# Thirty-two graph blocks through four layers on one core: bias sums, products and weight chunks take other places in the order

## The chip, the cores and the metric

The kernel runs on one core of one Trainium2 chip. Its time is the time on the device of one launch, in microseconds (us); lower is better.

## The reference

The input is x, 128 graphs of 64 nodes with 512 features, an adjacency matrix adj for each graph (symmetric in its pattern, with weights from 0.05 to 1), and a node mask of ones. Four layers follow, each with a norm, a relu and a residual; all in float32.

```python
def block(x, layer, ...):
    h = jnp.maximum(_layernorm(x, axis=-1), 0.0)
    return x + layer(h, adj, ...)

# layer 0
q, k = jnp.split(h @ Wqk, 2, axis=-1)
v = h @ Wv
agg = jnp.einsum('bij,bjd->bid', adj, k * mask[:, :, None])
w = inv_scale * mask * jnp.einsum('bid,bid->bi', q, agg)
out = jax.nn.softmax(w, axis=1)[:, :, None] * v
# layer 1: q, k, v with biases
weight = adj * jnp.exp(jnp.einsum('bqd,bkd->bqk', query, keyt))
weight = weight / jnp.sum(weight, axis=2, keepdims=True)
out = jnp.einsum('bqk,bkd->bqd', weight, value)
# layer 2: eight heads of 64, biases everywhere
scores = jnp.einsum('bhqd,bhkd->bhqk', q, k) * SCALE * (adj + adj)
out = softmax(scores) applied to v, then @ Wo.T + bo
# layer 3: graph diffusion of three hops
Xw = X @ Wv + bv
sj, si = Xw @ aw[:d, 0], Xw @ aw[d:, 0]
alpha = A * jnp.exp(leaky_relu(sj[:, None, :] + si[:, :, None] + ab[0]))
transition = alpha / (jnp.sum(alpha, axis=-1, keepdims=True) + 1e-12)
for k in range(3):
    H = H + Xk @ Wk[k] + bk[k]
    Xk = jnp.einsum('bij,bjd->bid', transition, Xk)
out = jax.nn.relu(H)
```

## The kernel before

The 8192 rows are cut into 32 blocks of 256 rows (four graphs), two tiles of 128 rows each (`TT`). `K` is 4, the number of chunks of 128 in 512 features; `F` is 256.

**Products.** A 512 x 512 weight times a block's activations is a `Product`: seven products of half size (Strassen's scheme in Winograd's form) instead of eight. VectorE and GpSimd make the sums of the operands (`sums` for the activations, `formed`, `later` and `chore` for the weights), TensorE does the seven products (L244 where the result is feature-major, L251 where it is row-major), and ScalarE, VectorE and GpSimd put the results together. A Product holds two PSUM banks, called ab and dc. Its first products are copied out (`keep_ab` L280 and L281, `keep_dc` L288), the banks take the later ones, and `store`, `store_T` or `add_to` (L302 to L341) empties them. `ps_mm` has four such banks, so the Product after the next waits until a Product's banks are empty. `ps_tr` and `ps_sc` have two banks each, for transposes and for scores and small sums.

**Order.** The program is written in the order in which blocks are to overlap: functions are generators or take lists `between`, whose entries are called at set places among the products of another block. A scheduler puts each engine's instructions in an order of its own; `tc.issue_after(i)` makes what is issued inside come after instruction i on its engine. Each engine works its list in order. All loads and stores named below go through SP's queue, in order as well: an issue that waits holds those behind it. Tiles with a tag share that tag's few buffers in turn.

**Start.** `prepare(0)` norms block 0; `transpose_weight` turns layer 0's q and k on TensorE (16 transposes, the four banks of results copied back by VectorE and ScalarE in turn, L420 and L422); `folded` multiplies them into one weight (pf, 32 matmuls, L430). `setup1` does the same for layer 1: its q and k are loaded, nine sums of products with the bias vectors are made on VectorE (L467: four for u, four for cc, one for d), then `transpose_weight` for q and for k, then `folded`. Layers 0 and 1 then run interleaved for pairs of blocks. `layer0` makes a masked adjacency am on GpSimd, its neighbour sums pa, gv, and a softmax whose end is `layer0_end`.

**Layer 2** is pipelined over blocks: `layer2_in` makes q and k of block b + 1, `layer2_scores` and `layer2_divided` its softmax, `layer2_context` and `out_part` what block b gives; the out product adds itself into x by `add_to` (L335 to L341, six operations on VectorE and GpSimd; the last on GpSimd is noted in `behind[0]`). Weight sums of later layers are done on GpSimd by `chore` (L99), one or two a block.

**Layer 3.** `setup3`, called at block 28 of layer 2, multiplies layer 3's Wv by the two halves of aw (pu, L754) to get two vectors us, stores them as a row and loads them spread over all partitions. A block then needs from Wv only four products hu (L788, two tiles by two vectors, each a sum along a row of h). `layer3_norm` loads x and adjT, norms x, makes the hu, and di and sj from them (L793, L800). `layer3_in` spreads di with a matmul (sm_i, L400), takes exp, multiplies by adjT to al (L816), then transposes h. `layer3_head` makes y2 and y1 of a block, `layer3_tail` y0 with den (L838) and the second hop (y<-po, L849), then y0's four VectorE stores (L858 to L862), `layer3_end` the last hop, the relu and out's store. In `layer3_step(b)` the norm is that of block b + 2, layer3_in that of b + 1 and layer3_end that of b - 1. The last blocks of layer 2 overlap the first of layer 3.

Of the kernel before, what the change touches and what calls it, by code (L numbers as in the profile page):

```python
# [13 lines left out]
P = 128  # L14
# [11 lines left out]
def kernel(ctx: ExitStack, tc: tile.TileContext, a: dict, out: bass.AP):  # L26
# [134 lines left out]

    def norm(x, name: str):
# [9 lines left out]
        nc.gpsimd.tensor_tensor(rstd, ve, neghalf, ALU.pow)  # L172
        nmr = small.tile([P, TT], FP, tag="nmr", name=f"nmr_{name}")
        nc.vector.scalar_tensor_tensor(nmr, mv[:, :, 0], -1.0, rstd, ALU.mult, ALU.mult)  # L174
# [48 lines left out]
    class Product:  # L223
# [109 lines left out]
        def add_to(self, x):  # L333
# [4 lines left out]
            nc.gpsimd.tensor_tensor(x[:, 1, :F], self.u3, x[:, 1, :F], ALU.add)  # L338
            nc.vector.tensor_tensor(x[:, 0, F:], self.c, x[:, 0, F:], ALU.add)
            nc.vector.tensor_tensor(x[:, 0, :F], self.a, x[:, 0, :F], ALU.add)  # L340
            nc.vector.tensor_tensor(x[:, 1, :F], self.d, x[:, 1, :F], ALU.add)  # L341
            behind[0] = nc.gpsimd.tensor_tensor(
                x[:, 1, F:], self.u3, x[:, 1, F:], ALU.add
# [67 lines left out]
    def transpose_weight(w, name: str):  # L411

        pts = [ps_mm.tile([P, K, P], FP, tag="mm", name=f"tw_{name}_{m}") for m in range(K)]
# [3 lines left out]
        for m, pt in enumerate(pts):  # L417
            flat = pt.rearrange("p k i -> p (k i)")
            if m % 2:
                nc.scalar.copy(w[:, m, :], flat)  # L420
            else:
                nc.vector.tensor_copy(w[:, m, :], flat)  # L422

    def folded(aT, bT, layer: int, place: int):

        m = slot(place, f"fold{layer}")
        for i in range(K):
# [7 lines left out]
            nc.vector.tensor_copy(m[:, quarters[i // 2][1], i % 2, :], pm[:, F:])  # L435
        return m

    def setup0():
# [4 lines left out]
        nc.vector.tensor_scalar(msc, mcol, -(float(D) ** -0.5), None, ALU.mult)  # L443
        return m, msc

    def setup1():
# [14 lines left out]
        for to, x, by in (  # L461
            *((u[:, k : k + 1], qT[:, k, :], 1) for k in range(K)),
            *((cc[:, k : k + 1], kT[:, k, :], 0) for k in range(K)),
            (d, None, 1),
        ):
            junk = med.tile([P, P, K], FP, tag="agg", name="bias1", bufs=2)
            nc.vector.scalar_tensor_tensor(  # L467
                junk, bias[:, 0] if x is None else x.rearrange("q (k p) -> q p k", k=K), 1.0,
                bias[:, by], ALU.mult, ALU.mult, accum_out=to,
            )  # L470
# [5 lines left out]
        for w, c in zip((qT, kT), "qk"):  # L476
            transpose_weight(w, f"{c}1")
        m = folded(kT, qT, 1, 2)
# [8 lines left out]
    def layer0(b: int, x, adjT, hs, hT, between):  # L487
# [3 lines left out]
        nc.gpsimd.tensor_tensor(  # L491
            am,
            adjT,
# [623 lines left out]
```

## Time and profile before

| | us |
|---|---|
| time, median of 3 runs | 2678.71 |
| lowest, highest run | 2675.41, 2680.66 |
| the profiled execution's own time | 2679.86 |
| its span | 2678.1 |
| TensorE busy in it | 2639.5 |
| VectorE, ScalarE, GpSimd busy in it | 1702.8, 947.7, 1288.7 |
| mean granted clock of TensorE | 0.996 |

The profile is of one execution: instructions of each engine with start and duration, what each waited for, and the clock granted to TensorE as a share of full speed. The page gives sums over the span. The view of waits gives, for an engine and line, the total time that it stood idle, what ended it, how many times, and the longest. The view by windows gives the busy time of PE (TensorE), PEld (its weight loads), DVE (VectorE), ACT (ScalarE) and POOL (GpSimd) in a stretch, then the granted clock, the DMA engines' share and GB/s. The timeline gives start, duration, engine, line and operation; brackets hold the idle time before it and what ended that. Names are those of the program without block numbers; q, k and v of the products are told by their suffix, as in u_y for a y product.

### The profile page before, as it was taken

What the parts mean: (1) busy time and instruction counts of PE and PEld (TensorE: products, weight loads), DVE (VectorE), ACT (ScalarE), POOL (GpSimd) and SP (SyncE); (2) the same over time, 40 slices, a digit from 0 to 9 for tenths busy, and PEclk for the clock granted to TensorE, in tenths of its full rate; (3) what the DMA queues carried; (4) which work ended last, traced back from release to release, by engine and by line L of the source; (5) the groups of instructions that cost most, each with busy time, mean ns of one, the idle gap of its engine ahead of it and who ended that gap; (6) DMA issues with size and microseconds to landing.
All of it is one profiled execution on the core that took longest, in us unless ns stands there. A gap on an engine that the chain in (4) does not pass through costs nothing.

```text
span 2678.1 us, 52780 instructions
## 1 busy us (share of the span) xinstructions
PE 2639.5 (99%) x20752; PEld 2253.1 (84%) x20752; DVE 1702.8 (64%) x4398; ACT 947.7 (35%) x2290; POOL 1288.7 (48%) x1585
## 2 busy tenths in 40 slices
PE   8999999999999999999999999999899999999999
PEld 5888888888888889999999999999777777777776
DVE  5566666666666676566566566566566666666664
ACT  2333334333333333333333333333323333333332
POOL 3443333333433335656655655655464444445544
PEclk9999999999999999999999999999999999999999
DMA  5200111111111122111111111111111111111110
GB/s 158 67 35 34 35 35 35 42 43 35 50 34 35 34 66 78 45 45 39 45 45 39 45 45 39 45 45 45 65 50 51 51 51 51 51 51 51 51 50 32
DMA packets 103165, 129.80 MB, mean 48 GB/s; under 512 B 40835, under 2 KB 50051, under 8 KB 102917
## 3 DMA queue, kind: packets, MB, share of 16 engines
q1 hardware_dynamic: 102340, 125.38, 13.9%
q8 instruction: 163, 2.67, 0.4%
q10 hardware_dynamic: 576, 1.05, 0.1%
q14 instruction: 86, 0.70, 0.1%
HBM read 76.07 MB, written 50.34 MB: 47 GB/s over the span
## 4 chain that ended last, share of the span: by engine, by line
PE 81%; POOL 6%; DVE 5%; DMA 4%; ACT 3%; issue 2%; ACTq 0%; POOLq 0%; SPq 0%; DVEq 0%
PE ab_v L251 11%; PE ab_y L251 9%; PE dc_v L251 8%; PE dc_y L251 6%; PE ab_g L244 4%; PE ab_k L244 4%; PE ab_g L251 4%; PE ab_q L244 4%; PE tr L190 3%; PE dc_g L244 3%; PE dc_g L251 3%; PE po L392 3%; PE dc_k L244 3%; PE ab_o L251 3%; PE dc_q L244 3%; DMA x<-x 2%
## 5 line engine op out<-in xcount | busy, mean ns | idle before, releaser
L179 ACT ACTIVATE h<-x,nmr,rstd 128x512 f32<-128x512 f32 x256 | 194.4, 806 | 219.6 <-DVE nmr L174 211.0
L172 POOL TENSOR_TENSOR rstd<-ve,neghalf 128x2 f32<-128x2 f32 x128 | 89.8, 701 | 365.6 <-DVE ve L170 365.4
L167 DVE BATCH_NORM_STATS2 stats<-x 128x6 f32<-128x512 f32 x256 | 165.3, 677 | 74.6 <-DMA x<-x 68.4
L251 PE MATMUL ab_y<-L_Wk,hT 128*128 128x256 f32 x768 | 207.5, 393 | 4.1 <-DVE u_y L303 2.6
L251 PEld LDWEIGHTS ab_y<-L_Wk,hT 128*128 128x128 f32 x768 | 136.4, 190 | 77.4 <-issue 25.2
L251 PE MATMUL ab_v<-L_Wv,hT 128*128 128x256 f32 x768 | 200.7, 384 | 0.0
L251 PE MATMUL ab_y<-L_Wk,S 128*128 128x256 f32 x768 | 197.8, 380 | 0.0
L251 PE MATMUL dc_v<-L_Wv,S 128*128 128x256 f32 x768 | 197.3, 379 | 0.0
L251 PE MATMUL ab_v<-L_Wv,S 128*128 128x256 f32 x768 | 197.1, 379 | 0.0
L251 PE MATMUL dc_y<-L_Wk,S 128*128 128x256 f32 x768 | 192.9, 380 | 1.3 <-DVE u_y L859 1.2
L251 PEld LDWEIGHTS dc_y<-L_Wk,S 128*128 128x128 f32 x768 | 145.2, 190 | 23.2 <-DVE u_y L859 3.7
L251 PEld LDWEIGHTS ab_v<-L_Wv,S 128*128 128x128 f32 x768 | 145.9, 190 | 19.8
L880 POOL TENSOR_TENSOR tz<-tz,y 128x512 f32<-128x512 f32 x63 | 91.5, 1452 | 146.0 <-ACT tz L877 146.0
L251 PEld LDWEIGHTS ab_y<-L_Wk,S 128*128 128x128 f32 x768 | 144.1, 191 | 18.5
L251 PEld LDWEIGHTS dc_v<-L_Wv,S 128*128 128x128 f32 x768 | 143.4, 190 | 18.9 <-issue 0.8
L251 PEld LDWEIGHTS ab_v<-L_Wv,hT 128*128 128x128 f32 x768 | 135.9, 190 | 15.4
L190 PE MATMUL tr<-ident,h 128*128 128x128 f32 x1024 | 134.4, 275 | 0.0
L190 PEld LDWEIGHTS tr<-ident,h 128*128 128x128 f32 x1024 | 119.5, 142 | 10.5
L216 POOL TENSOR_TENSOR S<-hT 128x256 f32<-128x256 f32 x128 | 101.1, 790 | 35.0 <-ACT hT L193 34.7
L219 POOL TENSOR_TENSOR S<-hT 128x256 f32<-128x256 f32 x128 | 107.9, 843 | 1.2
L306 POOL TENSOR_TENSOR gv<-u_g,p_g 128x256 f32<-128x256 f32 x32 | 23.4, 730 | 174.4 <-DVE u_g L303 174.4
L217 POOL TENSOR_TENSOR S<-S,hT 128x256 f32<-128x256 f32 x128 | 101.0, 789 | 11.6 <-DVE ve L170 10.3
(238 smaller groups left out, 6433.8 us busy)
## 6 DMA issues: line engine op xcount, KB each, us to landing
x<-x SPq DMA_DIRECT2D x128, 512.0 KB, 3.5
x<-in_x_dram SPq DMA_DIRECT2D x32, 512.0 KB, 3.6
out_dram<-x SPq DMA_DIRECT2D x31, 512.0 KB, 2.8
adjT<-in_adjT_dram SPq DMA_DIRECT2D x64, 64.0 KB, 1.9
adjq<-in_adj_dram SPq DMA_DIRECT2D x64, 64.0 KB, 2.3
L_Wk<-in_L_Wk_dram SPq DMA_DIRECT2D x16, 256.0 KB, 4.7
L_Wv<-in_L_Wv_dram SPq DMA_DIRECT2D x12, 256.0 KB, 5.3
q<-in_L_Wqk_dram ACTq DMA_DIRECT2D x4, 256.0 KB, 6.1
```

Of the source, the lines that this page charges most:

```text
L167: nc.vector.bn_stats(stats[:, t, :], x[:, t, :])
L172: nc.gpsimd.tensor_tensor(rstd, ve, neghalf, ALU.pow)
L179: nc.scalar.activation(h, x[:, t, :], AF.Relu, bias=nmr[:, t : t + 1], scale=rstd[:, t : t + 1])
L190: nc.tensor.transpose(pt[:, k, :], h[:, k * P : (k + 1) * P], ident)
L216: nc.gpsimd.tensor_tensor(S1, A21, A22, ALU.add)
L217: nc.gpsimd.tensor_tensor(S2, S1, A11, ALU.subtract)
L219: behind[0] = nc.gpsimd.tensor_tensor(S3, A11, A21, ALU.subtract)
L244: nc.tensor.matmul(dst[:, m * P : (m + 1) * P], w[:, place, k, m * P : (m + 1) * P], left[:, k, :], start=key not in self.begun, stop=last ...
L251: nc.tensor.matmul(dst, left[:, k, :], w[:, place, k, :], start=key not in self.begun, stop=last and k == 1, skip_group_check=True,)
L306: nc.gpsimd.tensor_tensor(y[:, 1, F:], self.u3, self.p5, ALU.add)
L392: nc.tensor.matmul(ps[t][half[g ^ t]], e[half[g], t, :], us[t][half[g]], start=True, stop=True)
L880: nc.gpsimd.tensor_tensor(tz[t], tz[t], y0[:, t, :], ALU.add)
```

## The change

- `setup1`: the nine bias sums are made earlier, in two groups with yields between them, so that the main loop can place them among the products of block 0; each reads a weight by columns. ScalarE copies all four banks of q's transposes; k's transposes go to `ps_tr` and `ps_sc` in turn. `layer0_end` of block 0 is called inside `folded`, after its first i.
- `transpose_weight` takes the places of its banks and which copies ScalarE does; layer 0's k uses two banks of `ps_sc` and two of `ps_mm`.
- `norm` keeps its first two small operations in `behind_norm`; msc (VectorE) and am (GpSimd) come after them.
- `add_to`: a's and d's adds come before c's; GpSimd's two adds of u3 change places.
- `setup3`: WvT is loaded as four chunks, two in one v buffer and two in agg buffers; the results of pu and pc go to two small tiles and are stored by two DMAs.
- Layer 3: `layer3_norm` is split; `layer3_dots` has the hu products, di and sj, and is issued behind the last VectorE store of y0. Both stages of `layer3_in` are called at the end of layer3_head's list. `layer3_tail` yields once more, before den. In the last three blocks of layer 2 the calls change places likewise: the first stage of layer3_in for block 0 goes into layer2_in's list, and block 2's dots come behind the last adds of out.

```diff
@@ -159,6 +159,8 @@
+    behind_norm = {}
...
@@ -169,9 +171,12 @@
         rstd = small.tile([P, TT], FP, tag="rstd", name=f"rstd_{name}")
-        nc.gpsimd.tensor_tensor(rstd, ve, neghalf, ALU.pow)
+        by_rows = nc.gpsimd.tensor_tensor(rstd, ve, neghalf, ALU.pow)
         nmr = small.tile([P, TT], FP, tag="nmr", name=f"nmr_{name}")
-        nc.vector.scalar_tensor_tensor(nmr, mv[:, :, 0], -1.0, rstd, ALU.mult, ALU.mult)
+        scaled = nc.vector.scalar_tensor_tensor(
+            nmr, mv[:, :, 0], -1.0, rstd, ALU.mult, ALU.mult
+        )
+        behind_norm.setdefault(0, (by_rows, scaled))
         hs = []
...
@@ -335,12 +340,12 @@
             nc.vector.tensor_tensor(self.u3, self.b, self.p1, ALU.add)
-            nc.gpsimd.tensor_tensor(x[:, 1, :F], self.u3, x[:, 1, :F], ALU.add)
-            nc.vector.tensor_tensor(x[:, 0, F:], self.c, x[:, 0, F:], ALU.add)
             nc.vector.tensor_tensor(x[:, 0, :F], self.a, x[:, 0, :F], ALU.add)
             nc.vector.tensor_tensor(x[:, 1, :F], self.d, x[:, 1, :F], ALU.add)
+            self.taken = nc.vector.tensor_tensor(x[:, 0, F:], self.c, x[:, 0, F:], ALU.add)
+            nc.gpsimd.tensor_tensor(x[:, 1, F:], self.u3, x[:, 1, F:], ALU.add)
             behind[0] = nc.gpsimd.tensor_tensor(
-                x[:, 1, F:], self.u3, x[:, 1, F:], ALU.add
+                x[:, 1, :F], self.u3, x[:, 1, :F], ALU.add
             )
...
@@ -408,20 +413,25 @@
-    def transpose_weight(w, name: str):
-        pts = [ps_mm.tile([P, K, P], FP, tag="mm", name=f"tw_{name}_{m}") for m in range(K)]
+    def transpose_weight(w, name: str, places=((ps_mm, "mm"),) * K, on_scalar=(1, 3)):
+        pts = [
+            pool.tile([P, K, P], FP, tag=tag, name=f"tw_{name}_{m}")
+            for m, (pool, tag) in enumerate(places)
+        ]
         for k in range(K):
...
             flat = pt.rearrange("p k i -> p (k i)")
-            if m % 2:
+            if m in on_scalar:
                 nc.scalar.copy(w[:, m, :], flat)
...
-    def folded(aT, bT, layer: int, place: int):
+    elsewhere = ((ps_tr, "tr"), (ps_sc, "sc")) * 2
+    def folded(aT, bT, layer: int, place: int, amid=lambda: None):
...
@@ -433,6 +443,8 @@
             nc.vector.tensor_copy(m[:, quarters[i // 2][1], i % 2, :], pm[:, F:])
+            if not i:
+                amid()
         return m
...
@@ -440,7 +452,8 @@
         msc = const.tile([P, n_tok // P], FP, tag="msc", name="msc")
-        nc.vector.tensor_scalar(msc, mcol, -(float(D) ** -0.5), None, ALU.mult)
+        with tc.issue_after(behind_norm[0][1].ins):
+            nc.vector.tensor_scalar(msc, mcol, -(float(D) ** -0.5), None, ALU.mult)
         return m, msc
...
@@ -458,24 +471,30 @@
         d = const.tile([P, 1], FP, tag="d1", name="d1")
-        for to, x, by in (
-            *((u[:, k : k + 1], qT[:, k, :], 1) for k in range(K)),
-            *((cc[:, k : k + 1], kT[:, k, :], 0) for k in range(K)),
-            (d, None, 1),
-        ):
-            junk = med.tile([P, P, K], FP, tag="agg", name="bias1", bufs=2)
-            nc.vector.scalar_tensor_tensor(
-                junk, bias[:, 0] if x is None else x.rearrange("q (k p) -> q p k", k=K), 1.0,
-                bias[:, by], ALU.mult, ALU.mult, accum_out=to,
-            )
+        def dots(*sums):
+            for to, x, by in sums:
+                junk = med.tile([P, P, K], FP, tag="e2", name="bias1", bufs=3)
+                nc.vector.scalar_tensor_tensor(
+                    junk, x, 1.0, bias[:, by], ALU.mult, ALU.mult, accum_out=to
+                )
+        def columns(w):
+            return [w[:, k, :].rearrange("q (k p) -> q p k", k=K) for k in range(K)]
+        dots((d, bias[:, 0], 1))
+        dots(*((u[:, k : k + 1], x, 1) for k, x in enumerate(columns(qT))))
+        yield
+        dots(*((cc[:, k : k + 1], x, 0) for k, x in enumerate(columns(kT))))
...
         nc.sync.dma_start(c1, crow.to_broadcast([P, D]))
-        for w, c in zip((qT, kT), "qk"):
-            transpose_weight(w, f"{c}1")
-        m = folded(kT, qT, 1, 2)
+        yield
+        transpose_weight(qT, "q1", on_scalar=range(K))
+        transpose_weight(kT, "k1", elsewhere)
+        m = folded(kT, qT, 1, 2, lambda: layer0_end(0, *softmax))
         formed(m, nc.gpsimd)
...
@@ -488,12 +507,13 @@
         am = small.tile([P, TT, N], FP, tag="am", name=f"am_{b}", bufs=2)
-        nc.gpsimd.tensor_tensor(
-            am,
-            adjT,
-            mcol[:, b * TT : (b + 1) * TT].unsqueeze(2).to_broadcast([P, TT, N]),
-            ALU.mult,
-        )
+        with tc.issue_after(behind_norm[0][0].ins):
+            nc.gpsimd.tensor_tensor(
+                am,
+                adjT,
+                mcol[:, b * TT : (b + 1) * TT].unsqueeze(2).to_broadcast([P, TT, N]),
+                ALU.mult,
+            )
         pa = [ps_tr.tile([P, D], FP, tag="tr", name=f"pa_{b}_{t}") for t in range(TT)]
...
@@ -738,25 +758,25 @@
         nc.sync.dma_start(ab, a["L3_ab"].to_broadcast([P, 1]))
-        halves = []
-        for i in range(2):
-            w = big.tile([P, K // 2, D], FP, tag="v", name=f"w3vT_{i}")
-            nc.sync.dma_start(
-                w,
-                a["L3_WvT"][i * D // 2 : (i + 1) * D // 2, :].rearrange("(k p) o -> p k o", p=P),
-            )
-            halves.append(w)
+        pair = big.tile([P, 2, D], FP, tag="v", name="w3vT")
+        chunks = [pair[:, k, :] for k in range(2)] + [
+            med.tile([P, D], FP, tag="agg", name=f"w3vT_{k}", bufs=2) for k in range(2, K)
+        ]
+        for k, w in enumerate(chunks):
+            nc.sync.dma_start(w, a["L3_WvT"][k * P : (k + 1) * P, :])
...
         for k in range(K):
-            for to, x in ((pu, halves[k // 2][:, k % 2, :]), (pc, bv[:, k : k + 1])):
+            for to, x in ((pu, chunks[k]), (pc, bv[:, k : k + 1])):
                 nc.tensor.matmul(to, aw[:, k, :], x, start=(k == 0), stop=(k == K - 1))
-        us2 = big.tile([2, D + 1], FP, tag="v", name="us2")
-        nc.scalar.copy(us2[:, :D], pu)
-        nc.scalar.copy(us2[:, D:], pc)
+        us2 = med.tile([2, D], FP, tag="h", name="us2", bufs=6)
+        cs2 = small.tile([2, 1], FP, tag="cc", name="cs2", bufs=1)
+        nc.scalar.copy(us2, pu)
+        nc.scalar.copy(cs2, pc)
         urow = tc.dram_tile([2, D + 1], FP, name="u3_row")
-        nc.sync.dma_start(urow, us2)
+        nc.sync.dma_start(urow[:, :D], us2)
+        nc.sync.dma_start(urow[:, D:], cs2)
         uc = const.tile([P, 2, D + 1], FP, tag="u3", name="u3")
...
@@ -775,12 +795,14 @@
         adjT = load_adjT(b, 3)
+        return x, adjT, norm(x, f"3_{b}")
+    def layer3_dots(b: int, x, adjT, hs):
         us, c3, _ = made3
-        hs = norm(x, f"3_{b}")
         sij = small.tile([P, 2, TT], FP, tag="sij", name=f"sij_{b}")
...
@@ -832,6 +854,7 @@
         p.second(ops, w3[0])
+        yield
         den = [ps_tr.tile([P, 1], FP, tag="tr", name=f"den3_{b}_{t}") for t in range(TT)]
...
@@ -859,9 +882,9 @@
         nc.gpsimd.tensor_tensor(y0[:, 1, F:], p.u3, p.p5, ALU.add)
-        nc.vector.tensor_tensor(y0[:, 0, F:], p.c, p.u2, ALU.add)
+        kept = nc.vector.tensor_tensor(y0[:, 0, F:], p.c, p.u2, ALU.add)
         nc.gpsimd.tensor_tensor(y0[:, 1, :F], y0[:, 1, :F], bs[:, :F], ALU.add)
-        yield r, y0
+        yield r, y0, kept
...
@@ -924,7 +947,7 @@
     turned(0)
-    transpose_weight(f0[1], "k0")
+    transpose_weight(f0[1], "k0", ((ps_sc, "sc"),) * 2 + ((ps_mm, "mm"),) * 2)
     m0, msc = setup0()
...
@@ -934,9 +957,13 @@
             fetch2(0)
+        between = [[], [chore], []]
+        if i == 0:
+            for n in (1, 2):
+                between[n].append(lambda: next(setup))
         if i == 1:
+            open_end.clear()
             made1 = next(setup)
-        between = [[], [chore], []]
         for n, end in open_end:
...
@@ -968,22 +995,32 @@
+        nonlocal normed3
         x, al, ops = made_in.pop(0)
...
             nonlocal normed3
-            next(stages, None)
             if b + 2 < n_blk and ahead:
...
-        y = layer3_head(b, ops, [[begin], [ending.pop()], [lambda: next(stages, None)]])
+        y = layer3_head(b, ops, [
+            [begin], [ending.pop()], [lambda: next(stages, None), lambda: next(stages, None)]
+        ])
         yield
         tail = layer3_tail(b, al, ops, y)
-        next(tail)
-        yield
-        r_y0 = next(tail)
-        ending.append(lambda: layer3_end(b, x, al, y, *r_y0))
+        for _ in range(2):
+            next(tail)
+            yield
+        r, y0, kept = next(tail)
+        ending.append(lambda: layer3_end(b, x, al, y, r, y0))
+        if b + 2 < n_blk:
+            with tc.issue_after(kept.ins):
+                if ahead:
+                    normed3 = layer3_dots(b + 2, *normed3)
+                else:
+                    normed3 = layer3_norm(b + 2, x2[b + 2])
         yield
...
@@ -1007,9 +1044,10 @@
             stages = layer3_in(0, *normed3, made_in)
-            next(stages)
         if b + 1 < n_blk:
-            qk, ops = layer2_in(b + 1, normed2[b + 1], [[], [lambda: chore(1 if b else 2)]])
+            qk, ops = layer2_in(b + 1, normed2[b + 1], [
+                [], [lambda: chore(1 if b else 2), lambda: next(stages, None)]
+            ])
         else:
...
@@ -1035,6 +1073,7 @@
             next(parts)
+            next(parts)
         (of_o,) = side_by_side(part)
...
@@ -1043,8 +1082,13 @@
             made3 = setup3()
-        if b >= n_blk - 3:
-            normed3 = layer3_norm(b - n_blk + 3, x2[b - n_blk + 3])
+        if n_blk - 3 <= b < n_blk - 1:
+            normed3 = layer3_dots(
+                b - n_blk + 3, *layer3_norm(b - n_blk + 3, x2[b - n_blk + 3])
+            )
+        elif b == n_blk - 1:
+            with tc.issue_after(of_o.taken.ins):
+                normed3 = layer3_dots(2, *normed3)
...
```

## The prediction

> **What bounds the kernel now.** I read the page, then TensorE's part of the view of waits, the granted clock in the windows around the long waits, and the timeline of one block of layer 3.
>
> ```profile
> PE 2639.5 (99%) x20752; PEld 2253.1 (84%) x20752; DVE 1702.8 (64%) x4398; ACT 947.7 (35%) x2290; POOL 1288.7 (48%) x1585
> ```
>
> TensorE is busy in 2639.5 of 2678.1 us, and the change removes no matmul. What an order can win is its 38.6 us of idle time, and time in which it is called busy but is slow. The waits name the idle time:
>
> ```profile
> PE tw_q L416 <- DMA q<-in_L_Wqk_dram: 6.1, 3, 5.6
> PE sm_i L400 <- DVE di L793: 3.4, 1, 3.4
> PE tw_k L416 <- DVE q L422: 3.3, 1, 3.3
> PE ab_y L251 <- DVE u_y L303: 2.6, 1, 2.6
> PE pu L754 <- DMA w3vT<-in_L_WvT_dram: 2.6, 1, 2.6
> PE tw_k L416 <- ACT q L420: 2.4, 2, 1.2
> PE tr L690 <- ACT hT L193: 1.7, 1, 1.7
> PE ab_k L244 <- DVE x L341: 1.7, 8, 0.2
> PE ab_o L251 <- DVE u_o L281: 1.5, 1, 1.5
> PE sm_w L400 <- DVE wd L518: 1.5, 1, 1.5
> PE dc_y L251 <- POOL L_Wk L99: 1.2, 1, 1.2
> PE dc_y L251 <- DVE u_y L859: 1.2, 2, 1.0
> ```
>
> Each line is one place, nearly all at seams between layers. Only the first, the load that opens the kernel, is out of the change's reach. The clock after two of these waits:
>
> ```profile
> 1884.00:1887.00 3.00, 1.09 (x3) 0.30 (x4) 0.00 (x0) 0.00 (x0) 1.52 (x2) 0.95 0.79 289
> 1887.00:1890.00 3.00, 3.00 (x9) 1.36 (x7) 0.00 (x0) 0.63 (x2) 0.00 (x0) 0.50 0.02 8
> 1921.00:1923.00 2.00, 2.00 (x10) 2.00 (x11) 1.86 (x3) 0.00 (x0) 2.00 (x2) 0.50 0.70 262
> ```
>
> The eighth column is the granted clock: 0.50 for about 3 us after pu's wait and after sm_i's. So a wait costs a tail too: ab_q x8 takes 1.91 and 1.57 us behind sm_i, against 1.06 elsewhere.
>
> One block of layer 3, its start taken as TensorE's den matmuls at 2203.11:
>
> ```profile
> 2204.62 1.29 DVE L167 BATCH_NORM_STATS2 stats<-x 128x6 f32<-128x512 f32 x2 [2.31 <-DMA x<-x]
> ...
> 2208.93 0.69 DVE L788 SCALAR_TENSOR_TENSOR hu<-h,u 128x512 f32<-128x512 f32 x1
> ...
> 2211.16 0.41 DVE L862 TENSOR_TENSOR y<-dc_y,u_y 128x256 f32<-128x256 f32 x1
> 2211.45 0.72 POOL L863 TENSOR_TENSOR y<-y,bs 128x256 f32<-128x256 f32 x1
> 2211.49 1.23 DVE L788 SCALAR_TENSOR_TENSOR hu<-h,u 128x512 f32<-128x512 f32 x1
> 2211.63 1.13 PE L251 MATMUL ab_y<-L_Wk,hT 128*128 128x256 f32 x4
> ```
>
> VectorE waits for the load of x two blocks ahead, then works in order through norm, three y sums, and y0's stores with two hu products between them. L862's end (2211.57) frees a bank, and TensorE's next ab_y starts 0.06 later. In every block ab_y stands 0.06 to 0.09 behind L862's end, between 8.37 us after den and 9.98. Periods run from 21.85 to 23.49, where the smallest seen is 21.78; 28 periods hold 9.1 us over that. The waits show little of it, since records of a late first matmul merge into its group.
>
> **The change part by part.**
>
> *Setup of layer 1 (42 to 73 us).* Nine bias sums (L467), pitch 0.96, fill VectorE from 46.37 to 54.96, ahead of the copies that empty tw_q's banks. TensorE's pf starts at 57.73, runs 15.40, and dc_g follows at 72.97. After: the sums stand between 18 and 41 us; ScalarE does q's four copies (0.52 pitch from 44.2), and k goes to other banks, so TensorE only needs tw_k's 2 us and the last k copy: pf at about 48.4. It then runs 13.93, as layer 0's pf did at 15.18, so it ends at 62.3; pa (1.09), now behind it, gives 63.4 against 72.97: 9.6 us. Its cover: the moved sums, 8 x 0.96, stand among block 0's copies. u_g's copy must end by 40.53 and I work out 40.25; each 0.96 that q's or k's load (issued by 32.8, 3.5 us to landing) comes late is lost in full. Bounds 7.5 and 10.3. The moves of msc and am beside the first norm meet no TensorE gap: nothing, up to 0.3 either way.
>
> *add_to.* In eight blocks of layer 2 with weight sums on POOL (L99), d's add (L341) waits for POOL's x add (L338) and TensorE's ab_k for L341. The waits show 1.7 us; the starts of ab_k are 29.10 apart there and 28.63 elsewhere, so the bound above is 8 x 0.47 = 3.8. d no longer waits for POOL; c does, for an earlier add. I take 3.0. POOL's two u3 adds swap, the same number; the store of x waits for the second as before.
>
> *Wv in four homes.* The second half's load waits for a buffer that TensorE frees, is issued at 1881.11, and pu waits 2.58 for it. After: two chunks lie in the buffer loaded from 1866.32, two in agg tiles loaded far earlier, so only pu's own work stays: 8.07 us from 1883.3 to the end of ab_k's first group become 3.5: gain 4.5 (2.6 if the tail stays). On SP the two bias row loads (bk) now stand behind the x store, and wait for pu; u's row goes in two stores, one 0.35 us issue more, ahead of u's load: u lands near 1889 as counted from the same pu, and its first reader, hu, comes at 1911. The Trainium skill's "DMA: Bandwidth & Descriptors" ("Rules for kernel authors", and the fit under "Anatomy of one DMA") speaks against it: small transfers should be joined, each having about 2 us fixed; four of 256 KB would be 4 x 2.6 against 2 x 3.2, 4 us more. The row: 512 KB land in 4.5, and all four chunks are issued 10 us or more before pu. On the path the rule would leave 0.5 of the 4.5; hidden, all stays. I take the row.
>
> *sm_i of block 0.* hu's place on VectorE stays, so ab_o's 1.47 stays. sm_i moves behind six more groups of TensorE (from 1917.4, to 1922.7), and di ends at 1920.7: the wait of 3.41 and its tail (0.39 + 0.85 + 0.51) go: 5.1. Next late: ab_k, which now comes at 1920.0, needs the bank that c's add of block 29 empties (L345, about 1918.8); then u_q's copy, needed by 1923, due at 1920.6.
>
> *The tails by two rules.* The Trainium skill's "TensorE: Matmul & The Clock Gate" ("What's actually happening") halves the clock after an idle window of about 3.4 us. By that only sm_i's wait has a tail, 1.75. In the rows pu's 2.58 also gives 0.50, and so does ab_y's 2.63 (0.65 over 2000 to 2004), while 1.47 and 1.73 give none. Tails by the rows: pf 1.5, pu 1.5, sm_i 1.75, ab_y 1.6, in all 6.3; by the rule alone 4.6 less. The measured durations decide.
>
> *Layer 2 to 3 (1960 to 2005).* 1.73 (tr behind a norm on ScalarE), 1.16 (POOL's weight sum), 0.82 (POOL S_c), 2.63 and its tail 1.6 (ab_y behind block 2's hu): 8 us. Block 2's norm and hu go behind out's stores, dc_o ahead of ab_o. I expect 1.73 and 4.2 to go, POOL's 2.0 to stay, and 1.4 to return: u_o's copy behind stats that wait for a load, or hu ahead of the next y's copies. 4.5, bounds 1 and 8.
>
> *Layer 3.* All four hu now stand behind L862: the last store comes 1.24 earlier (2 x 0.62), L859 0.62 earlier. Against it: di's two operations and al move past the next step's y2 stores, so SP's adjT load, which waits for al, stands between out's store and the x load. From 2220.18: y2's stores end 2221.27, di 0.2, hT 0.6, di 0.2, exp and its hand-over 0.4, al 0.25: 2222.95; then one issue, 0.4. The x load moves from 2222.94 to 2223.4, and 64 KB move ahead of its 512: later by d = 0.7 (0.4 to 1.2). With s = start of stats after den, u_y's copy (L281) ends at s + 9.79 before. di's two leave (-0.4); hu beside POOL costs 0.54 in the row above (1.23 against 0.69) and I count 0.9 with all four behind the stores (+0.36). It must end by 12.06, so a block stalls by s - (2.3 - d). (L859, by the same count, allows 2.37 - d: nearly equal.) Over the 27 s in the trace (mean 1.61, longest 2.97): stall left 3.6 at d = 0.7, 6.4 at 0.9, 2.0 at 0.5, against 9.1. Gain 5.5; I take 5. al ahead of y1's stores makes these 1.2 later, with over 4 us to the bank's next use.
>
> *Sum.* 9.6 + 3.0 + 4.5 + 5.1 + 4.5 + 5 = 31.7, less 2 for small waits that no view shows yet: 29.7. The profiled run's own time is 2679.86, 1.15 over the median: 2678.7 - 29.7 = 2649.
>
> **The rivals.**
> - *Layer 3 gains nothing or loses some.* d = 0.9 to 1.2 makes its share +2.7 to -5; with the rest: 2652 to 2660. For it: VectorE already waits 2.31 for x in each block, so that load carries the loop. Against: hu's 1.24 is more than d.
> - *The seams refill.* u_g's or k's copies late by two sums (2 us and a tail 1.5), and the 2-to-3 seam giving 1: 9 us back, 2658. For it: 0.2 us of slack at u_g. Against: the loads land before the sums begin.
> - *Slower: the x load held by adjT.* If al is so late that d = 1.9 (1.2 us more than I count, as when exp waits behind ScalarE's copies and adjT's 1.9 us to landing comes ahead of x), all 27 blocks stall, 33 us in all: layer 3 loses 24, all that the rest wins. Beyond that it is slower, 27 us for each further us. Against: exp stands ahead of y1's copy on ScalarE, and x does not wait for adjT to land.
> - *It doesn't do what it says.* If stats, not hu, set L862's lateness alone, layer 3 stays at 9.1 and the rest still gives 24: 2654.
>
> **How the numbers follow.** The sum as written, 2640 to 2655: 0.65. Layer 3 gaining nothing or a little lost: 0.17, and refilled seams 0.10, to 2663 together. Most of both: 0.02, still faster. No change within 0.2%, about 5 us and about what a measurement of this kernel can tell: 0.02. Slower by the x load: 0.04. The range 2639 to 2663 takes the first three less their ends. Faster 0.94, same 0.02, slower 0.04.
>
> **What would show it.** Right: pf starts near 48.4 at full clock and dc_g near 63.4; no wait of pu, none of sm_i; ab_k 28.63 apart throughout layer 2; layer 3's periods under 21.95, x loads 0.7 later against den. Wrong: TensorE waiting in each block of layer 3 for u_y L286 or L882, periods over 22; tw_k or dc_g late in setup; a wait over 2.5 us with a clock of 0.5 behind it at a new place.

## The result, and the profile after

| | before | after |
|---|---|---|
| median, fastest and slowest run, us | 2679.68 (2675.41 to 2681.00) | 2645.57 (2644.41 to 2646.76) |
| span of the profiled execution | 2678.1 | 2643.3 |
| TensorE busy in it | 2639.5 | 2624.6 |

The ratio is 0.9876 (95% interval 0.9864 to 0.9888): faster by 34.1 us, where 29.7 were forecast. (The median of before is over one run more than in the prediction.)

The busy times on the page of the kernel after:

```profile
PE 2624.6 (99%) x20752; PEld 2250.6 (85%) x20752; DVE 1695.9 (64%) x4396; ACT 950.4 (36%) x2292; POOL 1292.8 (49%) x1585
```

All of TensorE's waits in it (total, times, longest):

```profile
PE tw_q L424 <- DMA q<-in_L_Wqk_dram: 5.7, 3, 5.1
PE dc_y L256 <- DVE u_y L882: 3.1, 4, 1.1
PE ab_o L256 <- DVE u_o L286: 1.5, 1, 1.5
PE sm_w L405 <- ACT k L428: 0.6, 1, 0.6
PE ab_v L256 <- ACT qk L328: 0.4, 1, 0.4
PE ab_k L249 <- DVE v L310: 0.3, 1, 0.3
```

Fourteen causes have become six. The number of matmuls is the same, 20752, and still TensorE is busy 14.9 us less: of that, 6.7 us lie in the eight blocks of add_to and in layer 3, where the granted clock is 1.00 before and after, so this is waiting that the view does not name; 7.4 lie in the setup and at the seams, where the clock had been 0.50 for a time; the rest is the start.

Where the 34.8 us of span went is read from the starts of the same matmuls in the two timelines:

| from | to | before | after | gain | forecast |
|---|---|---|---|---|---|
| first matmul | pf of layer 0 | 9.47 | 8.71 | 0.8 (and 0.5 for an earlier first matmul) | 0 |
| pf of layer 0 | dc_g behind pf of layer 1 | 57.86 | 47.67 | 10.2 | 9.6 |
| third q of layer 2 | eleventh q | 232.80 | 229.02 | 3.8 | 3.0 |
| 29th q | scores of block 30 | 82.74 | 78.18 | 4.6 (pu) | 4.5 |
| scores of block 30 | scores of block 31 | 35.83 | 31.60 | 4.2 (sm_i) | 5.1 |
| scores of block 31 | den of block 2 | 87.69 | 82.11 | 5.6 (2 to 3) | 4.5 |
| den of block 2 | den of block 30 | 619.23 | 613.90 | 5.3 (layer 3) | 5 |

Layer 1's setup in the timeline of the kernel after (TensorE's pf and dc_g, ScalarE's copies of q, VectorE's of k):

```profile
43.67 2.05 ACT L428 COPY q<-tw_q 128x512 f32<-128x512 f32 x4 [2.11 <-PE tw_q L424]
43.75 1.91 PE L424 MATMUL tw_k<-ident,k 128*128 128x128 f32 x16
...
45.82 1.28 DVE L430 COPY k<-tw_k 128x512 f32<-128x512 f32 x2
46.27 0.49 PE L405 MATMUL sm_w<-wd,ones_bd 128*128 128x128 f32 x2 [0.60 <-ACT k L428]
46.59 13.97 PE L440 MATMUL pf<-q,k 128*128 128x512 f32 x32
```

TensorE does k's 16 transposes in one stretch, in 1.91 us; before, they were spread from 49.38 to 57.58. pf takes 13.97 where it took 15.40: the granted clock is 1.00 throughout it, and before it was 0.50 over pf's first 3 us.

pu, in TensorE's timeline:

```profile
1861.49 1.02 PE L772 MATMUL pu<-w3vT,aw 128*2 128x512 f32 x2
...
1864.22 1.02 PE L772 MATMUL pu<-w3vT,aw 128*2 128x512 f32 x2
1865.07 0.19 PE L772 MATMUL pc<-bv,aw 128*2 128x1 f32 x2
1865.19 1.16 PE L249 MATMUL dc_q<-S,L_Wq 128*128 128x128 f32 x8
```

All four chunks are there: the last landed at 1855.41. And layer 3 (first what TensorE waits for in the block with den at 1996.92, then VectorE and SP's issues in the next, den at 2019.34):

```profile
2004.74 1.13 PE L256 MATMUL dc_y<-L_Wk,S 128*128 128x256 f32 x4 [0.38 <-DVE u_y L882]
...
2016.69 0.38 DVE L838 TENSOR_TENSOR al<-di,adjT 128x128 f32<-128x128 f32 x1 [0.38 <-ACT di L836]
2017.11 0.37 SPq L63 DMA_DIRECT2D adjT<-in_adjT_dram  x1
2017.53 0.46 SPq L58 DMA_DIRECT2D x<-x  x1
...
2021.18 1.28 DVE L169 BATCH_NORM_STATS2 stats<-x 128x6 f32<-128x512 f32 x2 [2.58 <-DMA x<-x]
2025.83 0.41 DVE L882 TENSOR_TENSOR u_y<-ab_y,p_y 128x256 f32<-128x256 f32 x1
2026.68 0.42 DVE L885 TENSOR_TENSOR y<-dc_y,u_y 128x256 f32<-128x256 f32 x1
2027.02 0.68 DVE L810 SCALAR_TENSOR_TENSOR hu<-h,u 128x512 f32<-128x512 f32 x1
```

x is issued right behind adjT, and adjT right behind al: 1.81 us ahead of den, where it was mostly 2.1 to 2.2. Stats start 1.84 behind den, where it was 1.35 in the undisturbed blocks. And yet L885 ends 7.76 behind den, where L862 ended at 8.28 or later. 18 of the 28 periods are 21.77 or 21.78.

### The profile page after: what moved, and what is told of

Read it like the earlier page. It is cut to its first block, busy times and chain, and to the rows that moved or that the text cites. A ratio compares the mean times of both kernels' runs of the same rounds, so it can differ in the third digit from the quotient of the medians.

```text
span 2643.3 us, 52749 instructions
## 1 busy us (share of the span) xinstructions
PE 2624.6 (99%) x20752; PEld 2250.6 (85%) x20752; DVE 1695.9 (64%) x4396; ACT 950.4 (36%) x2292; POOL 1292.8 (49%) x1585
## 3 DMA queue, kind: packets, MB, share of 16 engines
HBM read 76.07 MB, written 50.34 MB: 48 GB/s over the span
## 4 chain that ended last, share of the span: by engine, by line
PE 93%; DVE 2%; DMA 2%; POOL 1%; ACT 1%; issue 0%; SPq 0%; ACTq 0%; POOLq 0%; DVEq 0%
PE ab_v L256 12%; PE ab_y L256 11%; PE dc_v L256 9%; PE dc_y L256 8%; PE ab_g L249 4%; PE ab_k L249 4%; PE ab_g L256 4%; PE ab_q L249 4%; PE tr L195 4%; PE ab_o L256 4%; PE dc_g L249 3%; PE dc_g L256 3%; PE po L397 3%; PE dc_k L249 3%; PE dc_q L249 3%; PE dc_o L256 3%
## 5 line engine op out<-in xcount | busy, mean ns | idle before, releaser
L904 DVE SCALAR_TENSOR_TENSOR x<-tz,x 128x512 f32<-128x512 f32 x64 | 44.3, 692 | 102.6 <-POOL tz L903 102.6
```

Of the source, the lines that this page charges most:

```text
L904: nc.vector.scalar_tensor_tensor(x[:, t, :], tz[t], 0.0, x[:, t, :], ALU.max, ALU.add)
```

## The experiments

Each kernel is the kernel after with one thing changed, and was run in three or five rounds beside the kernel before. Times of one kernel scatter over 1.5 to 4 us, in three kernels over 5.7 to 6.8, and the medians of before in these rounds lie 1.5 us apart, so differences of 4 us or less are read from the starts in the trace, stage by stage. A trace is of one execution.

**Layer 1's setup as before.**

```diff
-        dots((d, bias[:, 0], 1))
-        dots(*((u[:, k : k + 1], x, 1) for k, x in enumerate(columns(qT))))
-        yield
-        dots(*((cc[:, k : k + 1], x, 0) for k, x in enumerate(columns(kT))))
+        for to, x, by in (
+            *((u[:, k : k + 1], qT[:, k, :], 1) for k in range(K)),
+            *((cc[:, k : k + 1], kT[:, k, :], 0) for k in range(K)),
+            (d, None, 1),
+        ):
...
-        transpose_weight(qT, "q1", on_scalar=range(K))
-        transpose_weight(kT, "k1", elsewhere)
-        m = folded(kT, qT, 1, 2, lambda: layer0_end(0, *softmax))
+        for w, c in zip((qT, kT), "qk"):
+            transpose_weight(w, f"{c}1")
+        m = folded(kT, qT, 1, 2)
```

> The kernel after, with layer 1's setup as it was before (nine sums in one row on VectorE ahead of the copies of q and k, k's transposes in the four ps_mm banks, layer0_end of block 0 with the next step). Theory: the sums hold TensorE up alone, so this gives back what the trace shows between pf of layer 0 and dc_g behind pf of layer 1: 9.9 + 0.3 us, so about 2655.8, pf of layer 1 starting near 56.7 with half the clock for its first 3 us. Rival: part of the gain came from the start and from banks in other pools, and only the 3.3 + 2.4 + 1.5 of named waits return: about 2652.

2656.99 us, ratio to before 0.9918 (0.9902 to 0.9935): 11.4 more than the kernel after. From pf of layer 0 to dc_g it takes 10.5 more, and the old waits are back:

```profile
PE tw_k L424 <- DVE q L430: 3.3, 1, 3.3
PE tw_k L424 <- ACT q L428: 2.4, 2, 1.2
...
PE sm_w L405 <- DVE wd L532: 1.4, 1, 1.4
```

The theory holds for what is undone here as a whole: the sums, the banks and copies, and layer0_end with pa. The next run parts them. The rival, which counted named waits alone, does not hold: they make 7.1 of the 10.5.

**The sums moved, without the banks and copies.**

```diff
-        transpose_weight(qT, "q1", on_scalar=range(K))
-        transpose_weight(kT, "k1", elsewhere)
+        transpose_weight(qT, "q1")
+        transpose_weight(kT, "k1")
```

> The kernel after, but layer 1's q and k are transposed and copied as before (all eight banks from ps_mm, copies by VectorE and ScalarE in turn); only the bias sums, layer0_end and pa keep their new places. Theory: the sums were the nine and a half; without other banks TensorE waits about 1 us for q's copies before k's last transposes: + 1.0 to 1.5 between pf of layer 0 and pf of layer 1, 2647. Rival: the banks are half of the gain: + 4 or more, with a half clock in pf, 2650.

2648.00 (0.9879; 0.9866 to 0.9893), 2.4 more than after. In the trace k's transposes wait 1.52 for a q copy that stands on VectorE behind layer 0's agg products; pf to dc_g takes 2.3 more. So of the 10.5, some 8 go with the place of the sums, of layer0_end and of pa, which no run parts, and up to 2.3 with the other banks and ScalarE's copies. That share is rough: other kernels with the same setup as the kernel after take from 47.67 to 49.02 for the stage, which takes 49.95 here; the wait of 1.52 is the part that can be pointed at. I had put it at 1.0 to 1.5, and the rival's 4 is too much.

**add_to in its former order.**

```diff
+            nc.gpsimd.tensor_tensor(x[:, 1, :F], self.u3, x[:, 1, :F], ALU.add)
+            self.taken = nc.vector.tensor_tensor(x[:, 0, F:], self.c, x[:, 0, F:], ALU.add)
             nc.vector.tensor_tensor(x[:, 0, :F], self.a, x[:, 0, :F], ALU.add)
             nc.vector.tensor_tensor(x[:, 1, :F], self.d, x[:, 1, :F], ALU.add)
-            self.taken = nc.vector.tensor_tensor(x[:, 0, F:], self.c, x[:, 0, F:], ALU.add)
-            nc.gpsimd.tensor_tensor(x[:, 1, F:], self.u3, x[:, 1, F:], ALU.add)
             behind[0] = nc.gpsimd.tensor_tensor(
-                x[:, 1, :F], self.u3, x[:, 1, :F], ALU.add
+                x[:, 1, F:], self.u3, x[:, 1, F:], ALU.add
             )
```

> The kernel after, with the six adds of add_to in their former order. Theory: the eight blocks with weight sums on GpSimd go from 28.63 back to 29.10 each: + 3.8, so 2649.3. Rival: only the waits that the view shows return, 1.7: 2647.3.

2648.77 (0.9888; 0.9873 to 0.9903), 3.2 more; from the third to the eleventh q of layer 2 the trace has 3.70 more, and nothing more elsewhere in layer 2. The upper bound was the value: the waits that the view names, 1.7 in all before and 1.9 here, are only about half of it.

**Wv in two halves.**

```diff
-        pair = big.tile([P, 2, D], FP, tag="v", name="w3vT")
-        chunks = [pair[:, k, :] for k in range(2)] + [
-            med.tile([P, D], FP, tag="agg", name=f"w3vT_{k}", bufs=2) for k in range(2, K)
-        ]
+        for i in range(2):
+            w = big.tile([P, K // 2, D], FP, tag="v", name=f"w3vT_{i}")
...
+            halves.append(w)
```

> The kernel after, with layer 3's WvT again as two halves in v buffers. Theory: pu waits about 2.6 for the second half and what follows runs some 3 us at half the clock: + 4.5, 2650.1. Rival, by the rule of an idle window of 3.4 us: the wait has no tail at half clock, + 2.6 to 3: 2648.4.

2647.60 (0.9886; 0.9871 to 0.9901; its runs lie from 2645.7 to 2651.4), so the time alone decides little. The trace does: pu waits 2.29, and from the 29th q to layer 3's first den it takes 4.19 more.

```profile
1872.68 2.37 PE L774 MATMUL pu<-w3vT,aw 128*2 128x512 f32 x4 [2.29 <-DMA w3vT<-in_L_WvT_dram]
1874.98 0.80 PE L249 MATMUL dc_k<-S,L_Wk 128*128 128x128 f32 x2
1875.57 1.91 PE L249 MATMUL ab_k<-hT,L_Wk 128*128 128x128 f32 x8
```

The windows behind that wait (the eighth column is the granted clock):

```profile
1873.00:1876.00 3.00, 3.00 (x9) 1.19 (x7) 0.00 (x0) 0.62 (x2) 0.00 (x0) 0.65 0.31 111
1876.00:1879.00 3.00, 3.00 (x23) 3.00 (x23) 0.14 (x1) 0.37 (x1) 0.00 (x0) 0.78 0.32 92
```

ab_k x8 takes 1.91 instead of 1.06: in this execution the wait of 2.29 has its tail. It is also the slowest of the four; the others, at 2645.7 to 2647.8, have no trace, and whether their wait had a tail is not shown. Their times are nearer to the rival's.

**Layer 3's steps as before.**

```diff
         def begin():
...
+            if ahead:
+                next(stages, None)
             if b + 2 < n_blk and ahead:
-                normed3 = layer3_norm(b + 2, x2[b + 2])
+                normed3 = layer3_dots(b + 2, *layer3_norm(b + 2, x2[b + 2]))
...
             with tc.issue_after(kept.ins):
-                if ahead:
-                    normed3 = layer3_dots(b + 2, *normed3)
-                else:
+                if not ahead:
```

> The kernel after, with block b + 2's hu products in front of and among y0's stores and layer3_in's first stage at the head of the step, as before, in the steps from block 1 on. Theory: layer 3's periods are again 21.85 to 22.6, each set by y0's last store: + 5.3 over the 27 blocks, 2650.9. Rival: the load of x, 0.35 later in the kernel after, had eaten most of what the products' place gave, and the gain came with the seam: + 1 or less, 2646.5.

2654.12 (0.9910; 0.9896 to 0.9925), 8.6 more. From den of block 3 on it is 4.0 more over 27 periods, of which all but the last stand at 21.83 to 22.88 again. Its profiled execution is its slowest, and 6.0 of what it has more lie in the first two steps, where the old order meets the new seam: sm_i waits 2.01 and ab_y 2.48, each with a tail. The steady part was forecast at 5.3 and is 4.0 in this execution; kernels with the layer 3 of after differ by 1.5 over the same periods.

**hu behind the stores, layer3_in left at the head.**

```diff
         def begin():
...
+            if ahead:
+                next(stages, None)
             if b + 2 < n_blk and ahead:
                 normed3 = layer3_norm(b + 2, x2[b + 2])
```

> The kernel after, but layer3_in's first stage (sm_i, di, exp, al) stays at the head of the step as before; only the hu products stand behind y0's stores. Theory: al is early, so adjT and x are loaded as early as before (x 2.16 us ahead of den, stats at 1.35), y0's last two stores end 0.6 earlier than in the kernel after, and the 4.2 us of stall left in layer 3 fall to about 1: 2642.4. Rival: di's two operations, now between the two copies of y2 and y1 sums, and sm_i among y2's matmuls make u_y's copy the late one: 2646 to 2650.

2767.86: slower than before, 1.0327 (1.0312 to 1.0341). Neither line of the expectation holds.

```profile
PE sm_i L405 <- DVE di L815: 88.0, 30, 3.5
```

One of its blocks, VectorE and TensorE:

```profile
2197.37 0.68 DVE L810 SCALAR_TENSOR_TENSOR hu<-h,u 128x512 f32<-128x512 f32 x1
...
2198.12 0.28 DVE L815 TENSOR_TENSOR di<-eye,sij 128x128 f32<-128x128 f32 x1
2198.54 0.46 PE L405 MATMUL sm_i<-di,ones_bd 128*128 128x128 f32 x2 [2.85 <-DVE di L815]
...
2199.27 1.87 PE L256 MATMUL ab_y<-L_Wk,hT 128*128 128x256 f32 x4
```

And TensorE one block later, where the wait is a little longer and no slow matmul follows:

```profile
2225.16 0.46 PE L405 MATMUL sm_i<-di,ones_bd 128*128 128x128 f32 x2 [2.92 <-DVE di L815]
...
2225.89 1.03 PE L256 MATMUL ab_y<-L_Wk,hT 128*128 128x256 f32 x4
```

I had looked at VectorE, ScalarE and SP, and not at TensorE's own list. There sm_i stands among the next step's first y2 matmuls, and di, which it needs, is now made after y0's stores. TensorE waits about 3 in nearly every block (2.85 to 3.46 in 28 of the 30 waits). Behind two of three of these waits it then runs at half the clock for 3.41 us, and the period is 26.55 to 27.17; behind the others the clock stays at 1.00, and it is 24.87 to 25.04. So the wait costs about 3.2 over the shortest period of 21.78, and the half clock about 1.8 more. The mean of 27 periods is 26.1 instead of 21.9. The part of the change that looked like mere tidying, layer3_in moved to the end of layer3_head's list, is what lets hu move at all.

**layer3_in late, hu in front.**

```diff
             if b + 2 < n_blk and ahead:
-                normed3 = layer3_norm(b + 2, x2[b + 2])
+                normed3 = layer3_dots(b + 2, *layer3_norm(b + 2, x2[b + 2]))
...
             with tc.issue_after(kept.ins):
-                if ahead:
-                    normed3 = layer3_dots(b + 2, *normed3)
-                else:
+                if not ahead:
```

> The kernel after, but the hu products stay in front of and among y0's stores; only layer3_in's first stage is late. Theory: the x load and stats are 0.4 to 0.55 later with nothing gained at the stores, so every block of layer 3 stalls by about 0.4 to 0.6 more than before: 27 x 0.5 on top of undo_layer3's + 5.3: about + 17, 2662. Rival: a late al costs nothing, since x is loaded as soon as its buffer is free: the same as undo_layer3, 2651.

2675.05 (0.9986; 0.9979 to 0.9992): 29.5 more than after, 20.9 more than with both parts undone. Over the 27 periods from block 3 on it is 20.6 more than that kernel, 0.76 a block, where I had 0.5. Two terms make it: stats start at about 1.9 instead of 1.35, 0.55 later; and TensorE reaches ab_y 0.22 sooner than before (8.15 behind den instead of 8.37), since sm_i's 0.22 no longer stands among these matmuls. So late stats are dear, as the slower rival of the prediction said, and each half of the change loses without the other.

**adjT behind x.**

```diff
-        x = load_x(b, source, 3)
-        adjT = load_adjT(b, 3)
+        x = big.tile([P, TT, D], FP, tag="x", name=f"x3_{b}", bufs=4)
+        came = nc.sync.dma_start(x, tokens(source))
+        with tc.issue_after(came.ins):
+            adjT = load_adjT(b, 3)
```

> The kernel after, with adjT's load issued behind the x load of the same block, so that x does not wait for al. Theory: x is issued 2.16 us ahead of den again instead of 1.81 and stats start near 1.35 to 1.45 instead of 1.9; what is left of layer 3's stall, 4.2, falls to about 1: 2642.4. Rival: the long stats (2.3 to 2.9) that hold the last stalls come from the landing of x and not from its issue: 2645.

2646.45 (0.9876; 0.9861 to 0.9891): nothing. Stats do start earlier, at 1.2 to 1.5 in most blocks, but L882's equal still ends about 7.0 behind den. The block with den at 2019.19:

```profile
2020.48 1.29 DVE L169 BATCH_NORM_STATS2 stats<-x 128x6 f32<-128x512 f32 x2 [2.03 <-DMA x<-x]
...
2022.33 0.70 POOL L174 TENSOR_TENSOR rstd<-ve,neghalf 128x2 f32<-128x2 f32 x1 [1.78 <-DVE ve L172]
2023.06 0.16 DVE L176 SCALAR_TENSOR_TENSOR nmr<-mv,rstd 128x2 f32<-128x2 f32 x1 [0.81 <-POOL rstd L174]
2023.15 2.28 DVE L874 SCALAR_TENSOR_TENSOR y<-po,r,y 128x512 f32<-128x512 f32 x3
```

The scheduler, with x earlier, put nmr ahead of all three y sums. VectorE waits 0.81 there for GpSimd's power, and the 0.55 is gone. In the kernel after, one y sum fills that wait, as the block with den at 2019.34 shows: its y sum (L872) starts at 2022.91, nmr at 2023.76.

**The start undone.**

```diff
-        with tc.issue_after(behind_norm[0][1].ins):
...
-        with tc.issue_after(behind_norm[0][0].ins):
...
-    transpose_weight(f0[1], "k0", ((ps_sc, "sc"),) * 2 + ((ps_mm, "mm"),) * 2)
+    transpose_weight(f0[1], "k0")
```

> The kernel after, with msc and am in front of the first norm's small operations as before, and layer 0's k in the four ps_mm banks. Theory: the 0.76 us between the first matmul and pf of layer 0 return: 2646.3, to be seen in the trace more than in the time. Rival (the prediction): nothing, 2645.6.

2646.21 (0.9874; 0.9861 to 0.9887), within the scatter. pf of layer 0 starts at 15.77 here, but in the twelve other kernels that have the new start (after and eleven of those in this section) it starts anywhere between 13.46 and 15.59, and in before at 15.11. So 0.8 in the table can't be put down to the change; the forecast of nothing stands, as far as this can tell.

**The seams.**

```diff
         if n_blk - 3 <= b < n_blk - 1:
-            normed3 = layer3_dots(
-                b - n_blk + 3, *layer3_norm(b - n_blk + 3, x2[b - n_blk + 3])
-            )
+            with tc.issue_after(of_qk[b + 1][1].taken.ins):
+                normed3 = layer3_norm(b - n_blk + 3, x2[b - n_blk + 3])
+            with tc.issue_after(of_o.taken.ins):
+                normed3 = layer3_dots(b - n_blk + 3, *normed3)
```

> The kernel after, with hu of blocks 0 and 1 behind the last VectorE add of out, and the norm of those blocks behind the last q and k sums of layer 2. Theory: ab_o's wait of 1.5 (u_o behind hu) goes, and the 0.9 that blocks 30 and 31 lose to stats ahead of u_q: - 2.4, 2643.2. Rival: di of block 0 comes later by what hu is later and sm_i waits for it, over 2 us with half the clock behind: 2646 to 2649.

2646.03 (0.9871; 0.9857 to 0.9884): not to be told from after. The trace has 1.2 less up to layer 3's first den and 0.5 more in the next two periods: ab_o's wait is 0.6 instead of 1.5, and sm_i waits 0.3. A little of both theories.

**Both, and nmr behind the first y sum.**

```diff
-        return x, adjT, norm(x, f"3_{b}")
+        return x, adjT, norm_begin(x, f"3_{b}")
+
+    def layer3_normed(b: int, x, adjT, begun):
+        return x, adjT, norm_end(x, f"3_{b}", begun)
...
         next(tail)
+        if b + 2 < n_blk and ahead:
+            with tc.issue_after(hop[0].ins):
+                normed3 = layer3_normed(b + 2, *normed3)
```

`norm_begin` holds the norm down to rstd, `norm_end` nmr and h; hop[0] is a y sum of the second hop. The edits of "The seams" and of "adjT behind x" are in it too.

> As seams, and in layer 3 x is loaded ahead of adjT, and the last two steps of the norm (nmr and h) stand behind the first y sum of the second hop, so that VectorE does not wait for GpSimd's power between stats and the y sums. Theory: adjT behind x alone gave nothing, since its earlier stats (1.3 against 1.9) met VectorE's wait of 0.8 for GpSimd ahead of the y sums; with that wait gone y0's stores end 0.5 earlier than in the kernel after and layer 3's last 4 us of stall fall to about 1: 2640.3. Rival: the landing of x, late by up to 1.8 in single blocks, makes what stalls are left: 2643.

2640.15 (0.9850; 0.9836 to 0.9863): the fastest, 5.4 less than after, and its runs (2638.92 to 2641.31) lie below all of after's.

```profile
PE dc_y L263 <- DVE u_y L898: 1.2, 2, 0.8
...
PE ab_o L263 <- DVE u_o L293: 0.6, 1, 0.6
```

Of the 28 periods from block 2 on 26 are 21.77 or 21.78; the two others follow late x (stats at 3.3 and 3.0 behind den). In the second, x was issued in time and landed late, as the rival said. In the first, x was issued late: its issue waited 4.3 us for out's store to land. So the rival's word on the landing of x is true of 0.7 of the 1.8 us that are left, and the other 1.1 hang on the store.

**nmr alone.**

```diff
         next(tail)
+        if b + 2 < n_blk and ahead:
+            with tc.issue_after(hop[0].ins):
+                normed3 = layer3_normed(b + 2, *normed3)
```

> The kernel after, with the last two steps of layer 3's norm (nmr and h) behind the first y sum of the second hop as in best, but adjT loaded ahead of x as in the kernel after and the seams as there. Theory: stats at 1.9 still set the y sums and the first y sum stood ahead of nmr already, so alone this gives nothing, as adjT behind x alone gave nothing: 2645.6; both together give the 3 to 4 of best. Rival: the move of nmr and h alone made best's gain in layer 3: 2642.5.

2643.58 (0.9862; 0.9845 to 0.9878), the last edit without the seams and with adjT ahead of x. L896 (L882's equal) ends 4.86 behind stats instead of 5.06, and from block 2 to block 30 it is 1.5 less than after. So it gives something alone, less than with adjT behind x (2.4 in the same stretch): neither line held exactly. Differences of 1 us between executions are as large, so the split of best's gain stays rough.

## Why the prediction was right, point by point

- **Setup of layer 1** (9.6, found 10.2 in the trace and 10.5 when undone). pf started at 46.59, not 48.4: the copies ended sooner than I had put them. Of these 1.8, 1.3 are a sooner start of layer 0's pf; over the stage the sum is right.
- **add_to** (3.0, found 3.8). The mechanism was right; I took a middle value where the spacing of ab_k, 29.10 against 28.63 in eight blocks, already said 3.8.
- **Wv's chunks** (4.5, found 4.6). The rule of the Trainium skill against small transfers ("DMA: Bandwidth & Descriptors", Rules for kernel authors), by which I estimated that 0.5 of it would be left, cost nothing here: the loads are hidden, the last chunk landing 6.1 us before pu. (The page's fit is for DMAs issued by GpSimd; these are SP's.) As for the clock, an idle window of about 3.4 us ("TensorE: Matmul & The Clock Gate", What's actually happening), read as the length of a wait, would have left 2.6; the half clock behind 2.58 in before and behind 2.29 with two halves speaks for the rows. The gain of 4.6 holds for executions in which the wait has its tail.
- **sm_i of block 0** (5.1, found 4.2). The wait and its tail went. What came late next was not what I named: u_q (L315) stood behind stats of block 1, which wait 3.40 for a load, so ab_v waits 0.42 and more is lost in the group behind. The missing 0.9 is half of the 2 that I had set aside for small waits.
- **Layer 2 to 3** (4.5, found 5.6). Of the named waits only 1.1 (dc_y behind L882) came back, and the two waits for GpSimd, which I expected to stay, went as well; why, no run here shows.
- **Layer 3** (5, found 5.3). The x load came 0.35 later in issue and stats about 0.5 later; I had 0.7. But the working was wrong in two steps and came out right by luck. I had u_y's copy as the first to bind, at 12.06; the waits name L882. And I had L882's limit at 7.42 where TensorE now arrives at 7.28, because sm_i no longer stands in front of it. So a block stalls once stats start about 2.1 behind den (2.06 gave no stall, 2.12 one of 0.05), not 2.3; that stats moved by 0.5 and not by 0.7 made up for it. Its sums were a little off too: the 28 periods held 9.4 over 21.78 each, not 9.1, and the 27 starts of stats give 3.4 at d = 0.7, not 3.6.
- **The sum.** The six stages gave 33.7 where 31.7 was summed, and the 2 taken off for small waits was not needed on top: that is 4.0 of the 4.4 by which 34.1 exceeds 29.7.
- **The other rivals.** Layer 3 did gain, and by the products' place and not by stats alone, so neither "gains nothing" nor "doesn't do what it says" came; of the refilled seams (whose terms add up to 7, not 9) only the waits of 0.6 (sm_w), 0.42 and 1.1 came.
- **The slower rival** named the right place: late stats stall every block. al_back_only shows the slope, 0.76 a block for 0.55 later stats and 0.22 earlier matmuls. What I missed is a worse mishap next to it: with hu moved and sm_i left where it was, the change would have cost 88 us against before.

## What to carry to other kernels

When an operation is moved back on one engine, look up in every other engine's list where its reader stands, and move the reader too: hu moved alone cost 122 us against the pair, layer3_in alone 29. Price a stall by the period of the loop and by the granted clock behind it, not by the view of waits alone: here 19.9 us of idle time went and 14.9 more that had been called busy. And when a load is made earlier and nothing comes of it, look for what the scheduler then put in front: here a 0.8 us wait for another engine's small operation.

## What the runs showed of the hardware

Behind some of TensorE's waits the granted clock is 0.50 for 3.41 us, and the length of the wait alone does not say which. Single waits of 2.01, 2.10, 2.29, 2.48, 2.58, 2.63 and 3.41 had it behind them. But with hu moved alone nine waits of 2.85 to 3.18 had not, and in layer 1's setup in the kernel before it set in at 50.34, when no wait there had been longer than 1.45. Two windows of 3.41 us behind the waits of 2.85 and 2.92 shown above (the granted clock is the number behind the last bracket):

```profile
2199.30:2202.71 3.41, 3.41 (x10) 2.69 (x9) 0.32 (x2) 0.31 (x1) 0.00 (x0) 0.50 0.02 5
2226.60:2230.01 3.41, 3.41 (x20) 2.06 (x19) 0.68 (x2) 1.13 (x4) 0.00 (x0) 1.00 0.02 5
```

What the traces do show is a grid. A stretch at half clock lasts 3.41 us, or three times that in the setup, and within one trace the starts of these stretches lie whole multiples of 3.41 us apart (538, 10 and 23 times in before). If each trace is cut into such windows, the idle time inside one window tells the clock of the next: behind all 29 windows at full clock with 2.01 us or more of idle time the clock was 0.50, and behind none with 1.96 or less, leaving out the start and the end of the kernel. The wait of 2.85 has 2.65 in one window; that of 2.92 lies across a boundary, with 0.95 on one side and 1.96 on the other; in the setup several short waits add up to 2.27 in one window. The page "TensorE: Matmul & The Clock Gate" of the Trainium skill ("What's actually happening") gives a window of 3413 ns that runs free, and the grid agrees; its idle window of about 3.4 us asks for more than was needed here, 2.01 of 3.41. By this, a wait of 2 to 3.5 us can cost its tail at one time and not at another, as the wait for di did from block to block.
